# Four stacked graph layers on one core: another tile of each step goes to VectorE in layer 1, adjacency checks move from layer 1 to layer 3, constants are made one at a time, and layer 3's input relu goes to VectorE

## Chip, cores and metric

One core of one Trainium2 chip. The metric is device time in microseconds (us) of one launch; lower is better. Engines are named as the profile names them: PE is TensorE, with PEld for its weight loads; DVE is VectorE, ACT ScalarE, POOL GpSimd, SP SyncE, which here only issues DMAs.

## What is computed

The input is x (4096 rows of 64 features) and a dense float32 adjacency matrix adj (4096 x 4096, about one entry in a thousand is 1). Four layers, each `x = x + layer(relu(layernorm(x)), adj)`:

```
layer 0: h,q,k = lorentz linear maps;  att = adj * sigmoid((2 + 2 qm k^T)/scale + bias);  s = att h;  s / sqrt(|<s,s>|)
layer 1: w = mask * 0.5 ** (position counted from the row's last neighbour, the last 100 only);  w (h W) + bias
layer 2: 1 - 0.1 h - 0.01 * sum(h * (adj h))
layer 3: relu([h, (adj h) / max(deg, 1)] W^T)
```

## The kernel before

**Tiling.** Rows are in 32 tiles of 128; columns in 8 blocks of 512 (`NIB`), each with four row tiles (`CI`). The adjacency is loaded once as fp8 masks by POOL's DMA queue (`load_masks`, L186) and kept on chip for all layers. An fp8 mask is exact only if adj holds zeros and ones, so the kernel also reads adj again in float32 and checks it: `check` (L414) runs one VectorE instruction (L421) over a 128x1024 tile that SP's queue has fetched (L406; 512 KB, four buffers, so a tile is fetched once the check four before it is done). Layer 0 checks 60 tiles of half that size; 98 of full size remain for later. All must be done before `flagged` (L1237) sums the marks (`bad`, L1245), PE folds them over partitions (`pf`, L1249) and a flag decides whether a general version runs afterwards.

**Order.** The order of instructions on each engine is written out by hand. Epilogues of a block (`rows0`, `rows1`, `rows2`, `rows3`) are generators in a queue: `step` (L347) advances them piece by piece, and each engine runs what it is given strictly in that order. In layers 2 and 3, `beat` (L1499) runs after each four matmuls: a `step`, and a check if the list `often` says so for this beat.

**Layer 0** (0 to 297 us): scores on PE (L1015), sigmoids on ACT (L1028), masking on DVE (L1039), sums on PE (L1046). Early in it, `count_constants` (L896) makes the small matrices that layer 1 multiplies by (`after`, `beyond`, `pair`, `apart`, `later`, `lane`, `part`), mostly on POOL, in a burst of few pieces.

**Chunk counts** (297.9 to 314.7 us): `chunks_counted` (L1275) counts neighbours per block of rows on PE, for two halves of the columns. A dictionary says what is put in after which tile t: checks (`wide`), the three pieces of `weights_scaled` (L1292), and `all_taken`, which copies mask rows by SP's queue. `numbered` (L1346) then writes numbers into spare mask rows by DMA.

**Layer 1** (314.7 to 445.3 us): 264 units of one row tile and one column block, four to a step (k = 0 to 65), s = 0 to 3 in a step. For each step PE runs four `cnt` matmuls (L1391, in `counted`), then the four `acc` matmuls (L1423, in `products`) of the step before. Between them each `cnt` is rectified out of PSUM into int16, whose bits are the bf16 weights (`weights`, L1402): s = 1 by DVE (L1409; s = 3 too when k % 8 is 1), the others by ACT (L1411). The `cnt` tiles rotate through five PSUM banks, so unit n + 5 can only start once unit n is evacuated. After the products of a step comes a check if k is 4 or more and k % 5 is 0, 2 or 4, then a `step` for the epilogues.

**Layers 2 and 3** (445.3 to 511.7, then to the end): per layer 256 matmuls (L1509), each mask tile against features that are kept as a sum of two fp16 parts (`split`, L264). `rows2` (L1549) makes layer 3's input: it calls `norm` (L288) with `by_act`, where ACT takes the row sums (L296), the squares (L309) and the relu with its scale (L333, four instructions), before PE transposes (L1575). `rows3` (L1602) forms the output: ACT scales (L257), POOL adds twice (L261, L1617), DVE adds x (L1620), POOL issues the store (L1621).

The full-size checks by stage, counted from the code: 5 in the chunk counts, 38 in layer 1, 32 in layer 2, 23 in layer 3 (there one in three beats for the first 24 beats, then two in three).

Of the kernel before, what the change touches and what calls it, by code (L numbers as in the profile page):

```python
# [16 lines left out]
AF = mybir.ActivationFunctionType  # L17
# [9 lines left out]
P = 128  # L27
# [26 lines left out]
def kernel(  # L54
# [83 lines left out]
    def bc(col, r):  # L138

        return col.unsqueeze(2).to_broadcast([P, r, D])  # L140
# [4 lines left out]
    def model(general):  # L145
# [142 lines left out]
        def norm(rows, h, tag, table, up=UP, by_act=False):  # L288


            xr = x_sb[:, rows, :]
            st, va = small("st", tag), small("va", tag)
            sq = rows_tile("sq", tag)
            if by_act:
                for c in range(CI):
                    nc.scalar.activation(  # L296
                        sq[:, c, :], xr[:, c, :], AF.Copy, scale=-1.0 / D,
                        accum_out=st[:, c : c + 1],
                    )
            else:  # L300
                nc.vector.tensor_reduce(st, xr, AX.X, ALU.add)
                nc.vector.tensor_scalar(st, st, -1.0 / D, None, ALU.mult)  # L302
            yield
            xc = rows_tile("xc", tag)
            nc.gpsimd.tensor_tensor(xc, xr, bc(st, CI), ALU.add)  # L305
            yield
            if by_act:
                for c in range(CI):
                    nc.scalar.activation(  # L309
                        sq[:, c, :], xc[:, c, :], AF.Square, accum_out=va[:, c : c + 1]  # L310
                    )
            else:
                nc.scalar.activation(sq, xc, AF.Square)
                yield
                nc.vector.tensor_reduce(va, sq, AX.X, ALU.add)
            if table:
                yield
                rs = small("rs", tag)
                nc.scalar.activation(
                    rs, va, AF.Sqrt, bias=eps if up == 1.0 else eps_up, scale=1.0 / D / up / up  # L320
                )
                yield
                nc.vector.reciprocal(rs, rs)
            else:
                nc.vector.tensor_scalar(va, va, 1.0 / D / up / up, EPS / up / up, ALU.mult, ALU.add)
                rs = rsqrt(va, tag)
                yield
                yield
                yield
            h = xc if h is None else h  # L330
            if by_act:
                for c in range(CI):
                    nc.scalar.activation(  # L333
                        h[:, c, :], xc[:, c, :], AF.Relu, scale=rs[:, c : c + 1]
                    )
            else:
                nc.vector.scalar_tensor_tensor(h, xc, 0.0, bc(rs, CI), ALU.max, ALU.mult)
            yield
            return h

# [555 lines left out]
        def count_constants():  # L896
            tmp = epi.tile([P, 2, P], F32, tag="sup", name="tri")
            tri, diag = tmp[:, 0, :], tmp[:, 1, :]

            nc.gpsimd.memset(tri, 1.0)  # L900
            nc.gpsimd.affine_select(
                out=tri,
                in_=tri,
                compare_op=ALU.is_gt,
                fill=0.0,
                base=0,
                pattern=[[-1, P]],
                channel_multiplier=1,
            )
            nc.gpsimd.memset(part, 0.0)  # L910
            nc.gpsimd.memset(beyond, 0.0)
            nc.gpsimd.memset(pair, 0.0)
            nc.gpsimd.memset(apart, 0.0)
            nc.gpsimd.memset(later, 0.0)
            own = float(MAX_NEIGH * 128)
            for n in range(LANES):
                at = slice(n * NT, (n + 1) * NT)
                eye = ident[at, at]
                nc.gpsimd.tensor_scalar(pair[at, :], eye, 1.0, None, ALU.mult)
                nc.gpsimd.tensor_scalar(apart[at, at], eye, own, None, ALU.mult)  # L920
                if n > 0:
                    nc.gpsimd.tensor_scalar(apart[at, 0:NT], eye, -128.0, None, ALU.mult)
                yield
            yield
            yield
            nc.vector.tensor_scalar(diag, ident, float(MAX_NEIGH * 128), None, ALU.mult)
            nc.vector.scalar_tensor_tensor(after, tri, -128.0, diag, ALU.mult, ALU.add)
            nc.vector.memset(after[:, KEPT:P], 0.0)
            for q in range(QUAD):
                lanes = slice(q * NT, (q + 1) * NT)  # L930
                nc.gpsimd.tensor_scalar(beyond[lanes, lanes], tri[lanes, lanes], 1.0, None, ALU.mult)
                for n in range(LANES):
                    nc.gpsimd.tensor_scalar(
                        later[lanes, n * NT : (n + 1) * NT], tri[lanes, lanes], -128.0, None, ALU.mult
                    )
                nc.vector.memset(part[lanes, q : q + 1], 1.0)
            nc.vector.memset(lane, 0.0)
            nc.vector.memset(lane[:, NT - 1 : NT], 1.0)


        stream0 = pool("stream0", 1, l0) if general else None
# [460 lines left out]
        def weights(units, cnts, k):  # L1402


            ws = []
            for s, (cnt, (ib, t)) in enumerate(zip(cnts, units)):
                w = work1.tile([P, IB], I16, tag=f"w{s}", name=f"w_{ib}_{t}{sfx}", bufs=2)
                if s == 1 or (s == 3 and k % 8 == 1):
                    nc.vector.tensor_scalar(w, cnt, 0.0, None, ALU.max)  # L1409
                else:  # L1410
                    nc.scalar.activation(w, cnt, AF.Relu)  # L1411
                ws.append(w.bitcast(BF16))
            return ws

        with tc.manual_schedule():
# [34 lines left out]
            for _ in range(AHEAD):  # L1450
                fetch(2)
            chunks_counted(0, {
                0: wide, 2: scaled, 8: wide, 10: scaled,
                16: lambda: all_taken(range(QUAD, NIB)), 18: scaled, 22: wide,
            })
            chunks_counted(1, {4: lambda: numbered(0), 16: wide, 24: wide})
            if general:
# [6 lines left out]
            for blocks in GROUPS:  # L1464
                units = [(ib, t) for t in reversed(range(-1, NT)) for ib in blocks]
                for at in range(0, len(units), CI):
                    now = units[at : at + CI]
                    cnts = counted(now)
                    ws = weights(now, cnts, k)
                    if late is not None:  # L1470
                        products(*late)
                    late = now, ws
                    if k % 5 % 2 == 0 and k >= 4:
                        check(2)
                    k += 1
                    step()
                    if k == 4 and not general:
                        numbered(1)
                    if not moved and len(ready.get(1, ())) == NIB:
                        features_apart()  # L1480
                        moved = True
# [196 lines left out]
        with tc.manual_schedule():  # L1678
# [12 lines left out]
                for ib in range(NIB):  # L1691
                    degrees(ib)

            often[:] = [True, False, False]
            sums(3, s2a, v_sb3, done3, 4, 28)
            drain()
        l2.close()
# [55 lines left out]
```

## Time and profile before

| | us |
|---|---|
| median of 3 runs (585.33 to 585.69) | 585.34 |
| the profiled execution | 584.98 |
| its span | 583.2 |
| PE busy in the span | 558.3 (96%) |
| DVE / ACT / POOL busy | 461.7 / 364.6 / 256.7 |
| layer 1 (315 to 445): PE / DVE / ACT busy | 122.3 / 111.2 / 106.9 |

The span is the time from the first to the last instruction in the profile; 1.8 us lie around it. A group line names line, engine, operation, output and input, count, then busy time and mean ns, then the idle time of the engine just before, and what ended it. In a timeline, the first two numbers are start and busy time in us, and a bracket gives the idle time before it and its releaser. A matmul is shown as 0.38 us long, but back-to-back ones start 0.216 us apart: PE's idle in a bracket is 0.16 us less than what the wait costs.

### The profile page before, as it was taken

The numbers are of one execution on the slowest core, as the hardware profiler recorded it, in microseconds if no ns is written. First come the engines' busy times: TensorE is split into PE (matmuls) and PEld (weight loads), VectorE is DVE, ScalarE is ACT, GpSimd is POOL, SyncE is SP. The second block draws the span as 40 slices with busy tenths as digits, with TensorE's granted clock in tenths as the row PEclk, the third lists the DMA queues.
The fourth block names the chain that finished last, engine by engine and source line by source line (L and its number), as shares of the span: only waits on it lengthen the run. The fifth ranks groups of instructions, "written<-read, shape, count | busy, mean of one in ns | idle before, by whom it ended". The sixth has DMA issues, their size and how long they took to land.

```text
span 583.2 us, 8971 instructions
## 1 busy us (share of the span) xinstructions
PE 558.3 (96%) x2912; PEld 239.2 (41%) x2924; DVE 461.7 (79%) x867; ACT 364.6 (63%) x727; POOL 256.7 (44%) x483
## 2 busy tenths in 40 slices
PE   8999999999999999999989899999999999999995
PEld 3663333233333333333334345444444445444552
DVE  5779666788998999999965787979898888776742
ACT  3678667666776767667613788988784028863431
POOL 7625303976757575755346300201011336751360
PEclk9999999999999999999999999999999999999998
DMA  8995932699999999993243365545555797656921
GB/s 148 130 106 50 101 35 18 56 123 158 160 159 152 159 153 167 136 142 118 83 153 120 132 206 184 177 152 180 160 176 184 237 324 228 216 187 220 321 75 35
DMA packets 45417, 87.84 MB, mean 151 GB/s; under 512 B 6000, under 2 KB 24432, under 8 KB 45360
## 3 DMA queue, kind: packets, MB, share of 16 engines
q1 hardware_dynamic: 26112, 69.17, 36.2%
q0 software_dynamic: 18720, 17.57, 32.2%
q8 instruction: 25, 0.41, 0.3%
q10 hardware_dynamic: 528, 0.43, 0.3%
q14 instruction: 32, 0.26, 0.1%
HBM read 135.63 MB, written 1.05 MB: 234 GB/s over the span
## 4 chain that ended last, share of the span: by engine, by line
PE 57%; DVE 18%; POOL 9%; DMA 6%; ACT 5%; issue 4%; SPq 0%; ACTq 0%; DVEq 0%; POOLq 0%
PE acc L1046 14%; PE ps L1015 13%; PE acc L1509 9%; PE acc L1423 7%; PE cnt L1391 7%; DVE ckw L421 5%; DMA ckw<-adjt_dram 4%; DVE att L1039 3%; DVE w L1409 2%; POOL mask L186 1%; PE pt L247 1%; POOL s2a L267 1%; ACT ps L1028 1%; POOL xc L305 1%; DMA vec<-vecs_dram 1%
## 5 line engine op out<-in xcount | busy, mean ns | idle before, releaser
L421 DVE SCALAR_TENSOR_TENSOR ckw<-ckw 128x1024 f32<-128x1024 f32 x98 | 123.3, 1269 | 9.2 <-DMA ckw<-adjt_dram 5.4
L1015 PE MATMUL ps<-qt,kt 64*128 64x512 f32 x512 | 124.2, 611 | 4.1 <-DVE att L1039 3.1
L1046 PE MATMUL acc<-att,fb 128*64 128x512 f32 x512 | 117.8, 599 | 0.6 <-DVE att L1039 0.5
L1411 ACT ACTIVATE w<-cnt 128x512 int16<-128x512 f32 x184 | 97.1, 604 | 19.0 <-PE cnt L1391 18.1
L1039 DVE TENSOR_TENSOR att<-ps,mask 128x1024 f32<-128x1024 f32 x82 | 98.3, 1217 | 7.8 <-ACT ps L1028 7.8
L1028 ACT ACTIVATE ps<-ps,att_c,att_a 128x1024 f32<-128x1024 f32 x82 | 93.4, 1175 | 1.9 <-PE ps L1015 1.7
L1028 ACT ACTIVATE att<-ps,att_c,att_a 128x1024 f32<-128x1024 f32 x46 | 54.6, 1202 | 59.2 <-PE ps L1015 59.0
L186 POOL DMA_DIRECT2D mask<-adjt_dram x128 | 70.2, 560 | 19.5 <-DMA mask<-adjt_dram 17.6
L1015 PEld LDWEIGHTS ps<-qt,kt 64*128 64x128 f32 x512 | 44.8, 186 | 80.6 <-issue 33.5
L1391 PE MATMUL cnt<-mask,after 128*128 128x512 fp8e4 x256 | 67.1, 379 | 6.2 <-DVE w L1409 5.0
L1039 DVE TENSOR_TENSOR att<-att,mask 128x1024 f32<-128x1024 f32 x46 | 56.6, 1246 | 19.3 <-ACT att L1028 19.3
L1423 PE MATMUL acc<-w,s2a 128*128 128x512 bf16 x244 | 64.1, 379 | 1.5 <-ACT asb L231 0.8
L1046 PEld LDWEIGHTS acc<-att,fb 128*64 128x64 f32 x512 | 33.5, 136 | 73.0 <-issue 67.5
L305 POOL TENSOR_TENSOR xc<-x_sb,st 128x256 f32<-128x256 f32 x24 | 19.3, 802 | 95.8 <-DVE st L302 60.6
L1409 DVE TENSOR_SCALAR w<-cnt 128x512 int16<-128x512 f32 x72 | 48.5, 686 | 15.2 <-PE cnt L1391 14.9
L1509 PE MATMUL acc<-mask,s2a 128*128 128x512 fp8e4 x256 | 57.8, 379 | 0.0
L1509 PE MATMUL acc<-mask,s2b 128*128 128x512 fp8e4 x256 | 57.7, 379 | 0.0
L282 POOL TENSOR_TENSOR rs_a<-rs_y 128x4 f32<-128x4 f32 x48 | 19.1, 399 | 67.1 <-DVE rs_y L278 58.5
L421 DVE SCALAR_TENSOR_TENSOR ck<-ck 128x512 f32<-128x512 f32 x60 | 43.1, 719 | 0.0
L1391 PEld LDWEIGHTS <-after 128*128 128x128 bf16 x256 | 24.9, 99 | 36.6 <-issue 8.0
L1423 PEld LDWEIGHTS <-s2a 128*128 128x128 f16 x256 | 24.7, 98 | 31.5 <-issue 2.5
L1509 PEld LDWEIGHTS <-s2b 128*128 128x128 f16 x256 | 25.1, 98 | 27.1
(252 smaller groups left out, 633.3 us busy)
## 6 DMA issues: line engine op xcount, KB each, us to landing
ckw<-adjt_dram SPq DMA_DIRECT2D x98, 512.0 KB, 4.2
mask<-adjt_dram POOLq DMA_DIRECT2D x128, 128.0 KB, 8.5
ck<-adjt_dram SPq DMA_DIRECT2D x60, 256.0 KB, 5.6
x_sb<-x_dram SPq DMA_DIRECT2D x4, 256.0 KB, 7.6
out_dram<-y POOLq DMA_DIRECT2D x6, 128.0 KB, 2.4
apart_m<-mask SPq DMA_DIRECT2D x16, 16.0 KB, 3.9
mask<-apart_m SPq DMA_DIRECT2D x16, 16.0 KB, 4.8
out_dram<-y ACTq DMA_DIRECT2D x2, 128.0 KB, 2.1
```

The costliest lines, as they stand in the source:

```text
L186: nc.gpsimd.dma_start(out=masks[ib][:, g * CG : (g + 1) * CG, :], in_=adjt[ib, g])
L305: nc.gpsimd.tensor_tensor(xc, xr, bc(st, CI), ALU.add)
L421: nc.vector.scalar_tensor_tensor(at, at, 0.0, at, ALU.not_equal, ALU.not_equal, accum_out=odd[:, k : k + 1])
L1015: nc.tensor.matmul(ps[:, c, :], kt[half, g, :], qts[ib][half, :], start=True, stop=True)
L1028: nc.scalar.activation(to, ps, AF.Sigmoid, bias=att_c, scale=att_a)
L1039: nc.vector.tensor_tensor(att, frm, mask, ALU.mult)
L1046: nc.tensor.matmul(acc[c * D : (c + 1) * D, :], lhs[:, t, :], rhs[:, c, :], start=(at == 0), stop=(at == NG - 1), skip_group_check=True,)
L1391: nc.tensor.matmul(cnt, by, what, start=True, stop=True, skip_group_check=True)
L1409: nc.vector.tensor_scalar(w, cnt, 0.0, None, ALU.max)
L1411: nc.scalar.activation(w, cnt, AF.Relu)
L1423: nc.tensor.matmul(accs[ib], apart_s if t < 0 else both(s2a, t), w, start=(t == NT - 1), stop=False, skip_group_check=True,)
L1509: nc.tensor.matmul(acc, both(s2, t), masks[ib][:, t, :], start=(t == 0), stop=(t == NT - 1), skip_group_check=True,)
```

## The change

Six places. In layer 1, DVE takes s = 3 of each step and ACT the others (s = 1 goes to DVE too when k % 7 is 1). Layer 1 checks when k % 7 is 0, 2 or 4. In the chunk counts one check is left out, `all_taken` is put after tile 12 and the later two pieces of `weights_scaled` after tiles 20 and 28. Layer 3's first 24 beats check every second beat. `count_constants` yields after nearly every POOL instruction, takes `beyond` and `later` from `after`, and clears the last columns of `after` on POOL at its end. `norm` does the relu with its scale on DVE always (L337). Full-size checks by stage are then 4, 27, 32 and 35.

```diff
@@ norm
-            if by_act:
-                for c in range(CI):
-                    nc.scalar.activation(
-                        h[:, c, :], xc[:, c, :], AF.Relu, scale=rs[:, c : c + 1]
-                    )
-            else:
-                nc.vector.scalar_tensor_tensor(h, xc, 0.0, bc(rs, CI), ALU.max, ALU.mult)
+            nc.vector.scalar_tensor_tensor(h, xc, 0.0, bc(rs, CI), ALU.max, ALU.mult)
@@ count_constants
             nc.gpsimd.memset(part, 0.0)
-            nc.gpsimd.memset(beyond, 0.0)
-            nc.gpsimd.memset(pair, 0.0)
-            nc.gpsimd.memset(apart, 0.0)
-            nc.gpsimd.memset(later, 0.0)
+            yield
+            yield
+            yield
             own = float(MAX_NEIGH * 128)
+            nc.vector.tensor_scalar(diag, ident, own, None, ALU.mult)
+            nc.vector.scalar_tensor_tensor(after, tri, -128.0, diag, ALU.mult, ALU.add)
+            for q in range(QUAD):
+                lanes = slice(q * NT, (q + 1) * NT)
+                nc.vector.memset(part[lanes, q : q + 1], 1.0)
+            nc.vector.memset(lane, 0.0)
+            nc.vector.memset(lane[:, NT - 1 : NT], 1.0)
+            for to in (beyond, pair, apart, later):
+                yield
+                nc.gpsimd.memset(to, 0.0)
+            for q in range(QUAD):
+                at = slice(q * NT, (q + 1) * NT)
+                yield
+                nc.gpsimd.tensor_scalar(beyond[at, at], after[at, at], -128.0, None, ALU.is_equal)
+                for n in range(LANES):
+                    to = slice(n * NT, (n + 1) * NT)
+                    yield
+                    nc.gpsimd.tensor_scalar(later[at, to], after[at, at], 0.0, None, ALU.min)
             for n in range(LANES):
...
+                yield
                 nc.gpsimd.tensor_scalar(pair[at, :], eye, 1.0, None, ALU.mult)
+                yield
                 nc.gpsimd.tensor_scalar(apart[at, at], eye, own, None, ALU.mult)
                 if n > 0:
+                    yield
                     nc.gpsimd.tensor_scalar(apart[at, 0:NT], eye, -128.0, None, ALU.mult)
-                yield
-            yield
-            yield
...
+            yield
+            nc.gpsimd.memset(after[:, KEPT:P], 0.0)
@@ weights
-                if s == 1 or (s == 3 and k % 8 == 1):
+                if s == 3 or (s == 1 and k % 7 == 1):
                     nc.vector.tensor_scalar(w, cnt, 0.0, None, ALU.max)
@@ chunk counts
             chunks_counted(0, {
-                0: wide, 2: scaled, 8: wide, 10: scaled,
-                16: lambda: all_taken(range(QUAD, NIB)), 18: scaled, 22: wide,
+                0: wide, 2: scaled, 8: wide, 12: lambda: all_taken(range(QUAD, NIB)),
+                20: scaled, 28: scaled,
             })
@@ layer 1
-                    if k % 5 % 2 == 0 and k >= 4:
+                    if k % 7 in (0, 2, 4) and k >= 4:
                         check(2)
@@ before layer 3
-            often[:] = [True, False, False]
+            often[:] = [True, False]
             sums(3, s2a, v_sb3, done3, 4, 28)
```

## The prediction

> **What bounds the kernel now.** I read the busy shares first, then waits and timelines of the stretches that the change touches. PE is busy 96% and back to back from 60 us on but for short holes, so a microsecond counts where PE stands still, and nowhere else. The holes of layer 1, in the waits of 315 to 446 us:
>
> ```profile
> ACT w L1411 <- PE cnt L1391: 18.1, 44, 1.2
> DVE w L1409 <- PE cnt L1391: 14.9, 21, 2.5
> PE cnt L1391 <- DVE w L1409: 5.0, 7, 1.2
> ```
>
> Seven times PE waited for a tile that DVE evacuates, never for one of ACT's. With 0.16 us more each (pitch 0.216 against the 0.38 shown) that is 5.0 + 7 x 0.16 = 6.1 us. One of them in the timeline:
>
> ```profile
> 439.72 1.19 DVE L421 SCALAR_TENSOR_TENSOR ckw<-ckw 128x1024 f32<-128x1024 f32 x1
> ...
> 440.70 0.59 PE L1391 MATMUL cnt<-mask,after 128*128 128x512 fp8e4 x2
> 440.84 0.08 DVE L421 DVE_READ_ACCUMULATOR ckw<-ckw 128x1 f32 x1
> 440.84 0.42 DVE L337 SCALAR_TENSOR_TENSOR fa<-xc,rs 128x256 f32<-128x256 f32 x1
> 441.18 1.28 DVE L1409 TENSOR_SCALAR w<-cnt 128x512 int16<-128x512 f32 x2
> 441.18 0.60 ACT L1411 ACTIVATE w<-cnt 128x512 int16<-128x512 f32 x1 [0.64 <-PE cnt L1391]
> ...
> 441.91 0.59 PE L1391 MATMUL cnt<-mask,after 128*128 128x512 fp8e4 x2 [0.62 <-DVE w L1409]
> ```
>
> A check and an epilogue piece stand ahead of the evacuation on DVE; PE has two `cnt` and must wait for the bank of the third. The tail of the kernel, on DVE and PE:
>
> ```profile
> 556.82 0.43 DVE L1620 SCALAR_TENSOR_TENSOR y<-y,x_sb 128x256 f32<-128x256 f32 x1 [0.61 <-POOL y L1617]
> 557.17 1.22 DVE L421 SCALAR_TENSOR_TENSOR ckw<-ckw 128x1024 f32<-128x1024 f32 x1
> 558.31 0.08 DVE L421 DVE_READ_ACCUMULATOR ckw<-ckw 128x1 f32 x1
> 558.31 1.74 DVE L421 SCALAR_TENSOR_TENSOR ckw<-ckw 128x1024 f32<-128x1024 f32 x1
> 559.98 0.08 DVE L421 DVE_READ_ACCUMULATOR ckw<-ckw 128x1 f32 x1
> 560.66 0.43 DVE L1620 SCALAR_TENSOR_TENSOR y<-y,x_sb 128x256 f32<-128x256 f32 x1 [0.60 <-POOL y L1617]
> 563.53 0.42 DVE L1620 SCALAR_TENSOR_TENSOR y<-y,x_sb 128x256 f32<-128x256 f32 x1 [2.44 <-POOL y L1617]
> 563.88 0.41 DVE L1245 TENSOR_REDUCE bad<-odd 128x1 f32<-128x256 f32 x1
> ```
>
> And PE at the same time:
>
> ```profile
> 571.36 0.19 PE L1249 MATMUL pf<-one,bad 128*1 128x1 f32 x2
> 571.48 4.49 PE L1509 MATMUL acc<-mask,s2a 128*128 128x512 fp8e4 x20
> ```
>
> The last check ends at 560, `bad` at 564.3, and PE folds it at 571.36, with 20 matmuls behind it in its order. DVE is 7 us early.
>
> **Layer 1, the evacuations.** A `cnt` can be read about 0.47 us after its start (from 431.75 to ACT's start at 432.22, for one), DVE's evacuation takes 0.68, PE goes on 0.05 later: 1.20. Slot s = 1 gives its bank to the third `cnt` of the next step, nine matmuls on: 9 x 0.216 = 1.94, so DVE may be 0.74 late. Slot s = 3 is wanted first by its own product, twelve matmuls on: 2.59, so DVE may be 1.39 late. And of 38 checks (1.15 from start to start) 27 remain, no longer in consecutive steps: 12.7 us of DVE's 111 go. A step is 1.73 us; with one evacuation (0.60 from start to start), one check and a piece of 0.2 to 0.6 DVE is 0.2 to 0.6 late, inside 1.39. I let six of the seven waits go. At 414.9 ACT's evacuation of two finished sums (two of 0.70, to 415.4) is late next, and keeps 0.9 of that hole. Gain 6.1 - 0.9 = 5.2.
>
> The same move tightens ACT. Its three evacuations start 0.486 apart. Before it has slots 0, 2, 3; the tightest starts 0.06 late of an allowed 1.94 - 0.47 - 0.60 - 0.05 = 0.82. Now it has 0, 1, 2, and the third starts 2 x 0.486 - 2 x 0.216 = 0.54 late: 0.28 is left, and ACT regains 1.73 - 1.46 = 0.27 per step. What stands between its evacuations, in layer 1:
>
> ```profile
> L231 ACT ACTIVATE asb<-acc,level 128x512 f32<-128x512 f32 x8 | 5.1, 698 | 0.5 <-PE acc L1423 0.5
> L313 ACT ACTIVATE sq<-xc 128x256 f32<-128x256 f32 x7 | 3.0, 422 | 0.6 <-POOL xc L305 0.6
> L319 ACT ACTIVATE rs<-va,eps_up 128x4 f32<-128x4 f32 x6 | 1.9, 311 | 0.0
> L319 ACT ACT_TABLE_LOAD x1 | 1.3, 1283 | 0.0
> ```
>
> The table load with its root holds ACT from 365.26 to 366.76: evacuations 0.88 + 0.54 late of 0.82, a new hole of 0.6. Thirteen small pieces of 0.25 to 0.33 cost 0.05 each where alone, up to 0.3 where two meet or their input is late: 1.2 together. Three pairs of sums: 0.17 each, 0.5. So 2.3 comes back; bounds 0 (if DVE's better pace removes late inputs) and 4.7 (0.3 at each of twelve, 0.6, 0.5). Layer 1 by itself: 5.2 - 2.3 = **2.9 gained**, bounds 5.2 and 0.5.
>
> The row of the table load bears on a page: the Trainium skill, "ScalarE: Activation LUTs", section "What ACT_TABLE_LOAD costs", gives 1283 ns for the load and some 1380 ns of drain. Here the root starts 0.02 us after the load's end, so no drain shows; with one the new hole would be 2.0 and the layer's gain 1.5, and I go by the row.
>
> **Chunk counts.** PE stood still 0.97 us before `pw` (L1299) at 302.13, because DVE made `wn_size` only after a check that waited for its tile (to 301.86). With `pw` after tile 20, forty matmuls of 0.054 = 2.2 us later, its input is there. The chain behind it (counts, numbers, mask DMA to 316.3) moves along: SP's queue, free from 306.8, waits for DVE's numbers at 309.8, and `all_taken` leaves it earlier, not later. The left-out check ended at 306.1, before DVE was wanted. **1.0 gained**, bounds 1.3 and 0.2 (if the DMAs land no earlier).
>
> **Constants.** In layer 0 the burst sits on POOL from 104.7 to 108.5 and 110.9 to 116.2. ACT waited 2.97 us for `xc` (L305) behind its first part, and PE stood 0.73 + 0.16 before the scores at 111.95; DVE waited 2.04 for POOL's root behind the second, and PE lost 1.19 + 0.16 at 127.58 and some 0.6 in between. Singly, each piece (0.28, some 0.85) stands ahead of one mask DMA (0.56); masks are loaded some 20 tiles ahead, so that costs nothing unless a root is delayed, which could open one of the 0.8 us holes that later blocks show (180.97, 211.91, 242.86). **1.6 gained**, bounds 2.6 and -0.5.
>
> **The relu.** ACT's four take 1.07 (514.69 to 515.76), after a hop from DVE's reciprocal; on DVE, right behind it, one of 0.42 (the row of L337). Eight of them on DVE, 3 us, fit: DVE is busy 52 of 66 us in layer 2. On PE's path are only the transposes at 502.6 (0.47) and 515.3 (0.83 + 0.16, 0.15, and 0.25 for ACT's `asb` behind the relus). **1.0 gained**, bounds 1.5 and -0.6 (half a check ahead of it).
>
> **The moved checks.** Layer 3 has 35 instead of 23. Four more in its first 24 beats fit into DVE's idle time (3.6 us before 534.6, 1.4 before the first `y` at 549.1). The `y` of L1620 come 3.84 us apart while two checks stand between them (552.98, 556.82, 560.66), because POOL's add takes 1.59 beside a check and 0.72 alone. The changed order has two more after the `y` of 560.66, so the next is at 564.5; then seven in a row; then a `y`, and only then `bad`. From 564.85: 7 x 1.15 + 0.52 (one is stretched to 1.74 beside POOL) = 573.4; `y` 0.35, `bad` 0.41, hop 0.1: PE folds at 574.3 instead of 571.36, 2.9 late, and 20 matmuls wait. The tiles' DMAs can add: a load starts when the check four before has ended and lands 4.7 us later (median of 536 to 560; least 3.2), so the last check starts not before 568.8 + 4.7 = 573.5, and the hole is 4.2. I take **3.4 lost**, bounds 2.5 and 4.3.
>
> A page bears on the stretched rows too: "SBUF — State Buffer", section "Who interferes with whom", says that a DVE instruction with two SBUF inputs and a GpSimd one that reads SBUF exclude each other, and the later one is blocked outright. Here both lengthen (1.22 to 1.74 and 0.72 to 1.59). If only POOL paid, the hole would be 0.5 smaller.
>
> **Sum.** -2.9 - 1.0 - 1.6 - 1.0 + 3.4 = -3.1: 584.98 becomes 581.9 for an execution like the profiled one. The median lies 0.36 above it: **582.2**.
>
> **Rivals.**
> 1. The flag is not late (0.12): DVE's idle time in layer 3 before `bad` (3.8 before 534.6, 1.4, three of 0.6, 2.4: 9.4 us) takes nearly all twelve. For: 12 x 1.15 = 13.8 is only half again that. Against: most of the idle time lies before the order lets the last seven begin. 582.2 - 3.4 = 578.8.
> 2. ScalarE becomes layer 1's bound (0.17): its holes take what DVE's gave. For: 0.28 us of room. Against: no PE wait for ACT's `cnt` before. 582.2 + 2.9 = 585.1.
> 3. Slower (0.16): the late flag takes more than all gains. The place is `pf`; the price is 1.15 us for each check still open behind the `y` at 564.5. If the four extra checks of the first 24 beats are not absorbed, eleven are open, and the hole is 3.4 + 4 x 1.15 = 8.0: 582.2 + 4.6 = 586.8. It decides from a hole of 6.5, the sum of the gains. Against: 5 us of idle time in that stretch.
>
> **Numbers.** Forecast 0.55, rivals 0.12, 0.17, 0.16. Faster by over 0.2% (below 584.2; about what a measurement of this kernel can tell from no change): 0.55 + 0.12 = 0.67; within it 0.17; slower 0.16. All bounds at their best give 582.2 - 5.0 = 577.2, at their worst 590; leaving a tenth out on each side I say 578.5 to 586.8.
>
> **What would show it.** Right: PE's waits for DVE's `w` fall from 5.0 us to under 1, waits for ACT's `w` appear, one beside the table load; no hole at `pw`; ACT's `xc` wait near 110 gone; a hole of 2.5 to 4.3 before `pf`, and seven checks in a row ahead of `bad`. Wrong: no hole before `pf`, or PE waiting for ACT in most steps of layer 1.

## The result and the profile after

The changed kernel takes 589.67 us (median of 4 runs, 589.33 to 592.34), the kernel before 585.52 beside it: ratio 1.0080, 95% interval 1.0065 to 1.0094. The forecast was 582.2, with a range up to 586.8. The profiled execution took 589.73, its span 588.0, 4.8 longer than before. Stage times, here and below, are those of the one profiled execution of a kernel; where it lies far from the kernel's median, that is said. By stage, from the first matmul of each on PE (us):

| | before | after | difference | predicted |
|---|---|---|---|---|
| layer 0 ends at | 297.90 | 300.17 | +2.3 | -1.6 (constants) |
| chunk counts | 16.80 | 15.76 | -1.0 | -1.0 |
| layer 1 | 130.66 | 129.39 | -1.3 | -2.9 |
| layer 2 | 66.38 | 65.30 | -1.1 | -1.0 (relu, with the next row) |
| layer 3 until PE reaches `pf` | 59.53 | 58.47 | -1.1 | |
| PE idle ahead of `pf` | 0.09 | 5.60 | +5.5 | +3.4 |
| `pf` to the start of the last matmul | 4.23 | 5.72 | +1.5 | 0 |
| from there to the end of the span | 7.65 | 7.58 | -0.1 | 0 |

In what follows checks stand at L415 of the changed kernel, the rest of layer 1 where it stood. First layer 1, in the waits of 315 to 446 us:

```profile
DVE w L1409 <- PE cnt L1391: 28.9, 31, 2.9
ACT w L1411 <- PE cnt L1391: 16.6, 41, 1.5
...
PE acc L1423 <- ACT asb L231: 1.2, 6, 0.2
PE cnt L1391 <- ACT w L1411: 0.4, 1, 0.4
PE acc L1423 <- DVE w L1409: 0.2, 1, 0.2
PE cnt L1391 <- DVE w L1409: 0.2, 1, 0.2
```

DVE now waits for PE twice as long as before, and PE's waits for DVE's `cnt` fell from 5.0 to 0.2 us. Six waits for ACT's sums and one for ACT's `w` stand in their place; that one is beside the table load, where the prediction put it, and 0.36 long as shown (0.53 from start to start, with two of 0.27 behind it, where one of 0.6 was foretold). The timeline:

```profile
365.81 1.28 ACT L319 ACT_TABLE_LOAD   x1
...
367.11 0.30 ACT L319 ACTIVATE rs<-va,eps_up 128x4 f32<-128x4 f32 x1
...
367.31 3.02 ACT L1411 ACTIVATE w<-cnt 128x512 int16<-128x512 f32 x6
...
367.94 1.35 PE L1391 MATMUL cnt<-mask,after 128*128 128x512 fp8e4 x3 [0.36 <-ACT w L1411]
```

The tail, on DVE:

```profile
563.17 0.42 DVE L1620 SCALAR_TENSOR_TENSOR y<-y,x_sb 128x256 f32<-128x256 f32 x1 [0.61 <-POOL y L1617]
...
566.33 1.73 DVE L415 SCALAR_TENSOR_TENSOR ckw<-ckw 128x1024 f32<-128x1024 f32 x1
...
569.60 1.23 DVE L415 SCALAR_TENSOR_TENSOR ckw<-ckw 128x1024 f32<-128x1024 f32 x1 [0.39 <-DMA ckw<-adjt_dram]
...
571.52 1.22 DVE L415 SCALAR_TENSOR_TENSOR ckw<-ckw 128x1024 f32<-128x1024 f32 x1 [0.69 <-DMA ckw<-adjt_dram]
...
574.23 0.41 DVE L1245 TENSOR_REDUCE bad<-odd 128x1 f32<-128x256 f32 x1
```

And on PE:

```profile
574.69 0.19 PE L1249 MATMUL pf<-one,bad 128*1 128x1 f32 x2 [5.43 <-DVE bad L1245]
574.81 5.98 PE L1509 MATMUL acc<-mask,s2a 128*128 128x512 fp8e4 x20
```

Seven checks stand between the `y` and `bad`, as foretold, but they take longer, and the 20 matmuls behind `pf`, which took 4.49 before, take 5.98. The windows show the second (PE busy first; the granted clock is the third number from the end):

```profile
150.00:152.50 2.50, 1.87 (x6) 0.95 (x8) 2.50 (x5) 1.47 (x3) 2.08 (x6) 0.74 1.12 106
152.50:155.00 2.50, 2.50 (x10) 0.91 (x8) 1.99 (x4) 1.91 (x2) 2.07 (x7) 0.58 0.71 219
...
575.00:577.50 2.50, 2.50 (x7) 0.91 (x6) 0.91 (x3) 0.00 (x0) 0.90 (x2) 0.50 0.17 59
```

PE is busy all through 575 to 577.5, with 7 matmuls instead of 13: it runs at half its clock. In the kernel before the clock is 1.00 in every stretch of 2.5 us between 60 and 570 us. The other low stretch, near 150 us, lies behind the loss of layer 0:

```profile
140.06 0.69 POOL L922 TENSOR_SCALAR beyond<-after 32x32 bf16<-32x32 bf16 x1
...
140.81 0.60 POOL L186 DMA_DIRECT2D mask<-adjt_dram  x1
141.49 0.93 POOL L926 TENSOR_SCALAR later<-after 32x32 bf16<-32x32 bf16 x1
...
145.02 0.32 POOL L933 TENSOR_SCALAR apart<-ident 32x32 bf16<-32x32 f32 x1
145.27 0.64 POOL L305 TENSOR_TENSOR xc<-x_sb,st 128x256 f32<-128x256 f32 x1
...
145.94 0.42 ACT L313 ACTIVATE sq<-xc 128x256 f32<-128x256 f32 x1 [4.47 <-POOL xc L305]
...
148.73 1.13 PE L1015 MATMUL ps<-qt,kt 64*128 64x512 f32 x4 [2.06 <-DVE att L1039]
```

Five constant pieces, a mask DMA issue ahead of each, are queued on POOL in front of the centred rows `xc`: 5.9 us from the first issue at 139.37 to `xc`. In the kernel before five mask issues stand there alone, 2.7 us, and `xc` starts 0.64 earlier (144.63) although PE ran 2.7 us behind:

```profile
141.93 2.72 POOL L186 DMA_DIRECT2D mask<-adjt_dram  x5
...
145.33 0.42 ACT L313 ACTIVATE sq<-xc 128x256 f32<-128x256 f32 x1 [1.19 <-POOL xc L305]
```

In the changed kernel ACT's square waits for `xc`, the next sigmoids wait behind the square in ACT's order, DVE's masking waits for them, and PE stands still. Up to 138 us PE was those 2.7 us ahead of the kernel before; here it loses them and more: the hole and a second of 0.77 at 150.6 cost 3.2 us (with 0.16 more each), and the low clock behind them some 1.7 (2.5 us at 0.74 and 2.5 at 0.58).

**Theory** after these traces: constants made singly delay `xc` in a block of layer 0; seven checks behind the fifth `y` delay the flag; and a PE that stood idle is given half the clock for some microseconds afterwards, so a long hole costs more than itself. In layer 1 the thinner checks gain, and the move of the slot costs. **Rivals:** the holes of layer 0 come from the mask issues and not from the constants; the slot's move is free, or is itself the gain; the clock falls by its place in the program; the loss in the tail is one of DMA bandwidth, whatever the order.

### The profile page after: what moved, and what is told of

Its sections match the earlier page's. It is cut to its first block, busy times and chain, and to the rows that moved or that the text cites. A ratio compares the mean times of both kernels' runs of the same rounds, so it can differ in the third digit from the quotient of the medians.

```text
span 588.0 us, 8935 instructions
## 1 busy us (share of the span) xinstructions
PE 562.1 (96%) x2924; PEld 240.0 (41%) x2924; DVE 467.9 (80%) x872; ACT 357.8 (61%) x697; POOL 259.3 (44%) x484
## 3 DMA queue, kind: packets, MB, share of 16 engines
HBM read 135.63 MB, written 1.05 MB: 232 GB/s over the span
## 4 chain that ended last, share of the span: by engine, by line
PE 54%; DVE 16%; POOL 11%; DMA 8%; ACT 5%; issue 5%; SPq 0%; POOLq 0%; ACTq 0%; DVEq 0%
PE acc L1046 13%; PE ps L1015 12%; PE acc L1423 8%; PE cnt L1391 8%; PE acc L1509 6%; DVE att L1039 4%; DVE ckw L415 3%; DMA ckw<-adjt_dram 3%; POOL mask L186 2%; POOL x_sb L1566 2%; PE many L1280 1%; POOL prod L261 1%; POOL xc L305 1%; DMA ck<-adjt_dram 1%; DMA vec<-vecs_dram 1%
## 5 line engine op out<-in xcount | busy, mean ns | idle before, releaser
L415 DVE SCALAR_TENSOR_TENSOR ckw<-ckw 128x1024 f32<-128x1024 f32 x98 | 124.2, 1278 | 9.5 <-DMA ckw<-adjt_dram 5.8
L1411 ACT ACTIVATE w<-cnt 128x512 int16<-128x512 f32 x183 | 95.8, 604 | 17.2 <-PE cnt L1391 16.6
L1391 PE MATMUL cnt<-mask,after 128*128 128x512 fp8e4 x256 | 68.4, 379 | 2.3 <-DMA mask<-two 1.2
L1423 PE MATMUL acc<-w,s2a 128*128 128x512 bf16 x256 | 66.4, 379 | 1.4 <-ACT asb L231 1.2
L1509 PE MATMUL acc<-mask,s2a 128*128 128x512 fp8e4 x256 | 59.2, 386 | 0.0
L282 POOL TENSOR_TENSOR rs_a<-rs_y 128x4 f32<-128x4 f32 x48 | 17.7, 369 | 66.4 <-DVE rs_y L278 58.3
L415 DVE SCALAR_TENSOR_TENSOR ck<-ck 128x512 f32<-128x512 f32 x60 | 42.7, 712 | 0.0
L1423 PEld LDWEIGHTS <-s2a 128*128 128x128 f16 x256 | 24.6, 97 | 34.3 <-issue 6.9
L1509 PEld LDWEIGHTS <-s2a 128*128 128x128 f16 x256 | 25.0, 99 | 28.4 <-issue 1.9
```

The lines of the kernel that those rows point to most:

```text
L415: nc.vector.scalar_tensor_tensor(at, at, 0.0, at, ALU.not_equal, ALU.not_equal, accum_out=odd[:, k : k + 1])
L1391: nc.tensor.matmul(cnt, by, what, start=True, stop=True, skip_group_check=True)
L1423: nc.tensor.matmul(accs[ib], apart_s if t < 0 else both(s2a, t), w, start=(t == NT - 1), stop=False, skip_group_check=True,)
L1509: nc.tensor.matmul(acc, both(s2, t), masks[ib][:, t, :], start=(t == 0), stop=(t == NT - 1), skip_group_check=True,)
```

## Experiments

### Parts taken out of the change

**Constants in a burst, as before**, all else changed.

```diff
-(count_constants of the change)
+(count_constants of before)
```

> The changed kernel with the constants made in a burst again, as before the change. Theory A (in layer 0 the single constant pieces stand on POOL ahead of a block's xc, ACT waits 4.5 us for it, PE loses 4.9 us with the slower clock after it): the hole near 148 us goes, the two smaller ones near 112 and 127 come back (2.7 us), layer 0 ends at 297.9 instead of 300.2, and the time is about 587.4. Rival (the hole comes from the clock dip at 150 us, or from PE running 2.7 us ahead, whatever POOL does): a hole of 3 us or more stays near 150 us and the time is 589 or more.

Measured: 589.22 (588.99 to 590.38), ratio 1.0077 (1.0060 to 1.0094). ACT's wait of 4.47 and the hole near 148 are gone and the clock stays at 1.00 there; layer 0 ends at 298.77, 1.4 earlier. But PE then comes to `pf` earlier, the hole there is 6.55 instead of 5.60, and the medians differ by only 0.45, which the intervals don't tell from nothing. While the flag is late, the cure of layer 0 hardly shows.

**Checks as before**, all else changed.

```diff
-                    if k % 7 in (0, 2, 4) and k >= 4:
+                    if k % 5 % 2 == 0 and k >= 4:
-            often[:] = [True, False]
+            often[:] = [True, False, False]
```

> The changed kernel with layer 1's and layer 3's checks as before the change (38 and 24). Theory B (the twelve moved checks make the fold pf late by 5.6 us, and PE then runs its last 20 matmuls at half clock for another 1.4): the hole before pf is under 1 us and layer 3 is 6 to 7 us shorter; layer 1 gets some DVE waits back, 1 to 3 us; the time is 584 to 586. Rival (the moved checks cost nothing by themselves, layer 3 is longer because the relu now stands on DVE): the hole stays, about 589.

Measured: 588.15 (583.42 to 589.44, 10 runs), ratio 1.0024 (1.0001 to 1.0047). The hole ahead of `pf` is 0.09 and the matmuls behind it take 4.24: both losses of the tail go with the checks. But layer 1 takes 134.01, 4.6 more than in the change: one wait for DVE of 2.08 at 338.95, and behind it a low clock that costs 1.7. The profiled execution took 589.44, 1.3 above the median, and the ten lie far apart, so how often the wait comes is open; 584 to 586 was expected.

**The fold behind the last matmul** (PE issues `pf` five steps later).

```diff
-            for _ in range(steps):
+            for _ in range(steps + 5):
                 yield
             pf = pm.tile(...)
```

> The changed kernel, but PE folds the marks (pf) after its last matmul of layer 3 instead of 20 matmuls before; all checks stay where the change put them. Theory B (the cost is PE standing at pf): the matmuls of layer 3 end 6.5 to 7 us earlier, the time is 583 to 584. Rival (the checks' loads or DVE's lateness set the end themselves): the tail waits for DVE instead and the time is 587 or more.

Measured: 586.43 (584.98 to 589.59), ratio 1.0027 (1.0009 to 1.0045). The last matmul starts 8.8 us earlier, 1.75 of it from layer 0, but the rest from there takes 12.87 instead of 7.58: the last evacuations on ACT and DVE stand behind the flag in their order. From the start of layer 3 to the end the change takes 5.9 us more than the kernel before, and this one 3.9 more: a third of the loss was PE standing ahead of work that it could do, the rest is the flag itself. The time is short of the 583 to 584 foretold.

**More of the moved checks early in layer 3**: two beats in three from its start.

```diff
-            often[:] = [True, False]
+            often[:] = [True, True, False]
```

> The changed kernel with two checks in three beats from the start of layer 3 on (16 instead of 12 in the first 24 beats), so that about three instead of seven stand ahead of bad after the y of block 4. Theory B: each of the four costs 1.2 to 1.5 us at the end, so the hole before pf shrinks from 5.6 to about 0.5 us, the clock stays up, and the time is 583 to 585, if the first 24 beats have room on DVE. Rival (no room there: DVE or the loads are full, the lateness is only passed on): the hole stays over 3 us, 587 to 590.

Measured: 588.05 (586.64 to 589.16), ratio 1.0057 (1.0040 to 1.0073). The hole falls only to 3.47: between 529 and 556 DVE waits ten times for a tile, 5.2 us in all. Two of them, on DVE:

```profile
543.95 1.29 DVE L415 SCALAR_TENSOR_TENSOR ckw<-ckw 128x1024 f32<-128x1024 f32 x1 [1.05 <-DMA ckw<-adjt_dram]
...
556.15 1.48 DVE L415 SCALAR_TENSOR_TENSOR ckw<-ckw 128x1024 f32<-128x1024 f32 x1 [1.08 <-DMA ckw<-adjt_dram]
```

So the rival holds for a part: with two checks in three beats the tiles are late. Whether that is the DMA's bandwidth or the wait for a free one of the four buffers was not told apart; the DMA share from 529 to 556 is 0.91 here and in the change, 0.81 before.

### Parts put into the kernel before

**Constants alone.**

```diff
-(count_constants of before)
+(count_constants of the change)
```

> The kernel before with the constants made one at a time, and nothing else. Theory A: layer 0 loses the two holes near 112 and 127 us (2.7) and gets one near 148 (4.9 with the slow clock): about +2.2, 587.6. Rival (the hole needs other parts of the change): -2 to 0, 583 to 585.5.

Measured: 586.52 (585.31 to 589.18), ratio 1.0028 (1.0012 to 1.0044). The profiled execution has the wait of 4.45 at the square, the hole of 2.06 on PE and a clock of 0.68, 0.50 and 0.50 from 150 to 157.5; layer 0 ends at 302.62. That execution took 589.18, 2.7 above the median. The step that was to gain 1.6 loses 1.6 by itself, going by the ratio. How much depends on the clock: the six profiles with these constants end layer 0 at 298.42 and 298.59 where the clock stays up behind the holes, and at 299.64 to 302.80 where it falls, against 297.85 to 298.96 in the nine with the burst.

**The relu alone.**

```diff
-            if by_act: (four nc.scalar.activation)
-            else: nc.vector.scalar_tensor_tensor(h, xc, 0.0, bc(rs, CI), ALU.max, ALU.mult)
+            nc.vector.scalar_tensor_tensor(h, xc, 0.0, bc(rs, CI), ALU.max, ALU.mult)
```

> The kernel before with layer 3's input relu on DVE, and nothing else. If the relu is what made layers 2 and 3 up to pf 2.2 us shorter in the changed kernel: 583.3. If it was the thinner DVE queue at the end of layer 1: 585.0 to 585.5.

Measured: 582.54 (582.32 to 583.95), ratio 0.9959 (0.9946 to 0.9972). Layer 2 is 1.23 shorter, layer 3 1.05. In the timeline of the kernel before, on ACT and PE:

```profile
501.95 1.06 ACT L333 ACTIVATE sup<-xc,rs 128x64 f32<-128x64 f32 x4 [1.16 <-DVE rs L323]
502.59 0.81 PE L1575 MATMUL ph<-ident,sup 128*128 128x128 f32 x2 [0.31 <-ACT sup L333]
```

And with the relu on DVE:

```profile
500.95 0.52 DVE L331 SCALAR_TENSOR_TENSOR sup<-xc,rs 128x256 f32<-128x256 f32 x1
...
501.62 0.41 PE L1569 MATMUL ph<-ident,sup 128*128 128x128 f32 x2
```

The transposes find their input and PE doesn't wait. Layer 1, where no instruction differs, is 0.66 shorter here, 0.57 of it in the wait for the spare mask rows' DMA, and 0.07 shorter in another kernel with this edit: so much one profile differs from another.

**The slot alone.**

```diff
-                if s == 1 or (s == 3 and k % 8 == 1):
+                if s == 3 or (s == 1 and k % 7 == 1):
```

> The kernel before with DVE on the fourth tile of a step (and the second when k % 7 is 1), checks as before. If the later slot is what ended DVE's waits in layer 1: PE's waits for DVE's w fall below 2 us, ACT's tighter turn gives about 4 back, 584 to 585. If it was the eleven checks taken out of layer 1: DVE's waits stay, ACT's come on top, 587 or more.

Measured: 587.87 (586.92 to 589.70), ratio 1.0044 (1.0027 to 1.0061). In the profiled execution (589.70, 1.8 above the median) layer 1 takes 134.39, 3.7 more. PE's waits for DVE's `cnt` fall from 5.0 to 2.1, but that is one wait:

```profile
333.40 1.23 DVE L421 SCALAR_TENSOR_TENSOR ckw<-ckw 128x1024 f32<-128x1024 f32 x1 [1.87 <-DMA ckw<-adjt_dram]
...
334.89 1.28 DVE L1409 TENSOR_SCALAR w<-cnt 128x512 int16<-128x512 f32 x2
...
335.63 0.92 PE L1391 MATMUL cnt<-mask,after 128*128 128x512 fp8e4 x2 [2.10 <-DVE w L1409]
```

A check whose tile is late holds up DVE, with two evacuations behind it; and behind PE's wait the clock is 0.65 and 0.67 from 335 to 340, which costs another 1.7. The kernel with the checks of before and all else changed has the same wait at 338.95 and the same fall of the clock.

**The checks alone.**

```diff
-                    if k % 5 % 2 == 0 and k >= 4:
+                    if k % 7 in (0, 2, 4) and k >= 4:
-            often[:] = [True, False, False]
+            often[:] = [True, False]
```

> The kernel before with layer 1's checks thinned (k % 7) and layer 3's taken every second beat at first, as in the change, and nothing else; with the one check that the change leaves out of the chunk counts still there, 34 fall to layer 3. Layer 1 gains 2 to 4 us from a freer DVE. Theory B: the fold is late by 3 to 5 us and the slow clock costs 1.4 more: 586 to 589. Rival (the late fold needs the relu on DVE as well): 582 to 584.

Measured: 588.04 (586.75 to 589.25), ratio 1.0056 (1.0034 to 1.0078). Layer 1 takes 127.23, 3.4 less, with DVE still on its old slot; PE's waits for DVE's `cnt` are 1.5 instead of 5.0. The gain of layer 1 is that of the checks. The tail takes it back: a hole of 3.15 ahead of `pf`, and 5.92 instead of 4.23 behind it.

### Which version, and the clock by itself

**Relu and chunk counts in the kernel before.**

> The kernel before with two parts of the change: the relu of layer 3 on VectorE, and the new table of duties in the chunk counts (one check fewer there). Constants, layer 1 and its checks as before. Theory (the parts add up): the relu alone measured 0.9959 of before (2.4 to 2.9 us), the chunk counts took 15.76 instead of 16.80 us in every kernel that has the new table; the check that leaves them sits at the end, where the last check of before ended some 5 us ahead of the flag's multiply. So 2.5 + 1.0: 581.9 us if before is 585.4, no hole at the flag's multiply. Rival (the chunk's gain is taken back by the longer row of checks): 582.9, the same as the relu alone, with a hole ahead of the flag's multiply.

Measured: 582.04 (581.49 to 583.35), ratio 0.9946 (0.9932 to 0.9959). The chunk counts take 15.76, 1.0 less; by the ratios the pair gains 0.8 us on the relu alone, and 581.9 was expected. Within that the parts add up.

**With them, layer 1's checks thinned as in the change and put into layer 2.**

```diff
-        made, beats, often = [0], [0], [True, False]
+        made, beats, often = [0], [0], [True, True, False]
-                    if k % 5 % 2 == 0 and k >= 4:
+                    if k % 7 in (0, 2, 4) and k >= 4:
```

> The kernel before with the relu on VectorE, the new table in the chunk counts, and the thinner checks in layer 1 (three beats in seven), the displaced ones put into layer 2 at two beats in three instead of one in two; layer 3's checks as before, so none is issued behind the fifth y. The tile that VectorE evacuates in layer 1 stays the second; constants as before. Theory (the thin checks are the gain in layer 1, and the flag is late only because the displaced checks stand in layer 3): layer 1 takes about 127 us (130.0 in the relu kernel, 127.2 with thin checks alone), no hole ahead of the flag's multiply, the last 20 matmuls in about 4.2; layer 2 pays 0 to 1.5 us. Time 578.5 to 581 us. Rival (VectorE is the bound of layer 2 too, 24.5 of 30 us busy there): layer 2 pays what layer 1 gains, 3 us, and the time stays at 581.5 to 582.5.

Measured: 592.48 (591.10 to 593.22), ratio 1.0126 (1.0111 to 1.0140). Layer 1 takes 128.06, of which 0.86 are four matmuls of layer 2 that the profile shows ahead of its last product: 127.2, 3.4 less than without the move. No hole stands ahead of `pf`; but layer 2 takes 75.11 instead of 65.29. The theory left this out, and the rival was far too mild. Where it is lost first:

```profile
478.35 0.17 DVE L1558 TENSOR_SCALAR inn<-inn 128x4 f32<-128x4 f32 x1
...
480.15 0.26 ACT L296 ACTIVATE sq<-x_sb 128x64 f32<-128x64 f32 x1 [6.12 <-POOL x_sb L1560]
...
481.12 0.67 ACT L231 ACTIVATE asb<-acc,level 128x512 f32<-128x512 f32 x1
...
481.84 1.11 PE L247 MATMUL pt<-ident,asb 128*128 128x128 f32 x4 [4.18 <-ACT asb L231]
```

Five checks in a row (469.81 to 477.5, one of them with a tile 1.01 late) stand ahead of `inn`; POOL's new x waits for `inn`, ACT idles 6.12 before its row sums, and the evacuation PE waits for stands behind these in ACT's order. From 480 to 487.5 the clock is 0.57, 0.50 and 0.57. Layer 2 has no room for so many checks. Later holes of this kernel, of 1.99 at 501.4 and 2.48 at 522.5, are followed by the full clock.

**Matmuls that fill the wait ahead of `pf`.** The changed kernel with 24 more matmuls, whose result nothing reads:

```diff
+            fill = pm.tile([P, IB], F32, tag="pr", name="fill")
+            for _ in range(24):
+                nc.tensor.matmul(fill, both(s2a, 0), masks[0][:, 0, :], start=True, stop=True, skip_group_check=True)
             pf = pm.tile(...)
```

> The changed kernel with 24 matmuls of 128x512 more, whose result nothing reads, issued just ahead of the flag's multiply (about 5.2 us of TensorE work at the full clock); all else is as in the change. The flag stays as late as it is, but TensorE doesn't stand idle while it waits. Theory (idle time ahead of the flag lowers the granted clock, and so costs more than itself): the hole of 5.6 us is filled for the most part, the 20 matmuls behind the flag's multiply take 4.2 to 4.6 us instead of 5.98, no clock of 0.50 is seen there, and the time is 1.0 to 1.6 us below the changed kernel's. Rival (the clock falls by something else than the idle time, such as the place in the program): the 20 matmuls take 5.9 again, and the time is that of the changed kernel or higher by what the fillers overhang.

Measured: 588.90 (588.70 to 591.19), ratio 1.0067 (1.0052 to 1.0083). The profile of PE, and below it that of the windows:

```profile
568.62 5.34 PE L1250 MATMUL fill<-mask,s2a 128*128 128x512 fp8e4 x24
575.50 0.19 PE L1255 MATMUL pf<-one,bad 128*1 128x1 f32 x2 [1.54 <-DVE bad L1245]
575.62 4.49 PE L1515 MATMUL acc<-mask,s2a 128*128 128x512 fp8e4 x20
```

```profile
575.00:577.50 2.50, 2.00 (x11) 1.01 (x12) 1.30 (x5) 0.00 (x0) 1.29 (x2) 1.00 0.16 56
577.50:580.00 2.50, 2.50 (x13) 0.98 (x10) 0.04 (x1) 0.00 (x0) 0.00 (x0) 1.00 0.19 62
```

The program differs only in that PE is busy, and stands idle 1.54 instead of 5.43 as shown; the 20 matmuls take 4.49 at the full clock: it is the idle time that lowers it, not the place in the program. A check's tile came 1.71 late in this profile, and the flag with it (65.36 us from the start of layer 3 to `pf` instead of 64.07), so that of the 1.5 us saved behind `pf` 0.2 is left; another 0.5 by which the profile is shorter lies in layer 0. The medians differ by 0.8, where 1.0 to 1.6 was foretold.

**Single constants at half the pace**, in the kernel before: each `yield` of the new `count_constants` stands twice.

> The kernel before with the constants made singly as in the change, but one in every second step instead of in each, so that about half as many pieces and mask issues stand on GpSimd ahead of a block's centred rows; all else as before. Theory (the pieces and the mask issues between them hold up the centred rows, and so ScalarE and TensorE): of the wait of 4.5 us that ScalarE had at the square near 145 us at least 1.5 us goes, the hole on TensorE there falls from 2.7 to below 1.5 us, the granted clock stays at full speed behind it, and layer 0 ends at 295.5 to 297.5 us (297.9 before, 302.6 with a piece in every step): time 583.0 to 585.0. Rival (another cause than the pieces, for instance the mask issues alone): hole and end of layer 0 stay as with a piece in every step, 298.5 or later.

Measured: 586.72 (586.06 to 590.28), ratio 1.0027 (1.0015 to 1.0039); in the profiled execution (590.28, 3.6 above the median) layer 0 ends at 303.47. The theory's times were wrong, its mechanism not: ACT's wait near 145 falls from 4.45 to 2.15 and PE's hole there to 0.77, but pieces are now left for the next block:

```profile
177.74 0.60 POOL L186 DMA_DIRECT2D mask<-adjt_dram  x1
...
178.41 0.60 POOL L305 TENSOR_TENSOR xc<-x_sb,st 128x256 f32<-128x256 f32 x1
...
179.05 0.42 ACT L313 ACTIVATE sq<-xc 128x256 f32<-128x256 f32 x1 [5.04 <-POOL xc L305]
...
181.84 1.24 PE L1031 MATMUL ps<-qt,kt 64*128 64x512 f32 x4 [2.69 <-DVE att L1055]
```

The hole moved from 149 to 181 us with the pieces; the clock behind it is 0.55, 0.50 and 0.59 from 182.5 to 190. In the kernel before no piece is left by then, and that block's hole is 0.62. Five mask issues stand ahead of `xc` with and without the pieces, and the hole comes with the pieces: so the pieces make it. What the issues add to it was not tried apart.

**Half of the checks moved**: relu, chunk counts, and a check at every second step of layer 1 (31 instead of 38), the rest in layer 3.

```diff
-                    if k % 5 % 2 == 0 and k >= 4:
+                    if k % 2 == 0 and k >= 4:
-            often[:] = [True, False, False]
+            often[:] = [True, False]
```

> The kernel before with the relu on VectorE and the new table in the chunk counts (the pair that measured 0.9946), and layer 1's checks at every second step from the fourth on (31 instead of 38), no two in consecutive steps; layer 3's first 24 beats check every second beat, as in the change. Slots and constants as before. Three checks are then left behind the fifth y and the sixth y no longer stands ahead of the marks' sum, against seven and a y in the change. Theory (VectorE's waits in layer 1 go with the checks, and each check behind the fifth y costs TensorE 1.15 us once the slack of the flag is used up): layer 1 about 128.5, the hole ahead of the flag's multiply 5.6 - 4 x 1.15 - 0.35 = 0.6, no low clock behind it; against the pair's 582.04, 2.0 less in layer 1 and 0.5 more at the flag: 580.5. Rival (the moved checks load the DMA queues too, and the last tiles land late whatever their number): the hole is 2 to 3 us, the clock falls behind it, and the time is 583 to 584.

Measured: **579.60** (578.90 to 580.21), ratio 0.9892 (0.9874 to 0.9910): 1.1% faster than before. Layer 1 takes 127.93. On DVE and PE:

```profile
563.18 1.74 DVE L415 SCALAR_TENSOR_TENSOR ckw<-ckw 128x1024 f32<-128x1024 f32 x1
...
564.96 0.42 DVE L1239 TENSOR_REDUCE bad<-odd 128x1 f32<-128x256 f32 x1
```

```profile
566.09 0.19 PE L1243 MATMUL pf<-one,bad 128*1 128x1 f32 x2
566.21 4.49 PE L1503 MATMUL acc<-mask,s2a 128*128 128x512 fp8e4 x20
```

Three checks behind the fifth `y`, none of them waiting for its tile; `bad` is ready 0.7 us before PE comes to `pf`.

**The change without the slot and the constants.**

> The change without its two parts that are held to have lost: VectorE keeps the second tile of a step in layer 1, and the constants stay in their burst. It has the thin checks in layer 1, the denser ones in layer 3, the table of the chunk counts and the relu on VectorE. Beside the kernel that has the change but for the constants it tells the move of the slot by itself. Theory (the slot's move costs in layer 1 because ScalarE's three consecutive tiles leave it no room): layer 1 takes 127.0 to 128.1 instead of 129.3, the hole ahead of the flag's multiply stays at 5 to 6.5 us with a low clock behind it, and the time is 585.5 to 588. Rival (the slot's move is free, the loss lies in the late flag and the clock alone): layer 1 takes 129 to 130.

Measured: 586.79 (585.16 to 588.71), ratio 1.0019 (1.0005 to 1.0032). Layer 1 takes 126.52, against 129.30 in the kernel that differs by the slot alone (the first experiment): a difference of 2.8. Of that 0.7 is PE's wait for the spare mask rows' DMA (0.45 here, 1.15 there), so the move costs 2.1; the other kernels with thin checks and the old slot, where that wait is 1.16 and 1.12, took 127.2 both, 2.1 less than 129.30. The hole ahead of `pf` is 6.45 and the clock 0.50 behind it:

```profile
570.37 0.19 PE L1243 MATMUL pf<-one,bad 128*1 128x1 f32 x2 [6.29 <-DVE bad L1239]
570.49 6.95 PE L1503 MATMUL acc<-mask,s2a 128*128 128x512 fp8e4 x20
```

## Why the prediction was wrong

The predicted sum was -3.1, the profile has +4.8. The 7.9 between them, from the table of stages:

1. **"Singly, each piece ... stands ahead of one mask DMA ...; ... so that costs nothing unless a root is delayed"** failed: 3.9 of the 7.9 (+2.3 for -1.6). The gains came (2.7 us by 138), but the new holes cost 3.2 and the clock behind them some 1.7, and what was delayed is no root. It is `xc`, for which ACT had waited 2.97 in the very row that the prediction read. The pieces meet the next `xc` instead, with a mask issue between each two, and hold it for 4.47. The bound of 0.5 for a loss was taken from existing holes of 0.8 and not from the length of the queue.
2. **The moved checks: mechanism right, size wrong**: 2.1 (5.5 for 3.4). The `y`s came 3.84 apart and seven checks stood in a row, as foretold. But PE came 0.9 nearer, since the relu shortens PE's part of layer 3 and not the chain of the `y`s; and the checks took 10.4 us from the last `y` instead of 8.6, two stretched beside POOL for one, and two late tiles (0.39 and 0.69). The late tile was in the prediction's bound of 4.3, PE's approach was not. The prediction took its rows of a check and POOL's add for "both lengthen", as if against the rule that the later one is blocked; in order of time these rows fit that rule. POOL's add at 564.48 runs to 565.32, the check of 564.66 ends at 566.40, the next add (565.39) at 566.98 and the next check (566.33) at 568.06, each some 0.6 (add) or 1.1 (check) behind the end of the one before: so a check pays for each add begun before it, and two adds stretched two checks. The third rival ended on the right side by luck: its four extra checks were absorbed (seven in the row, not eleven), and it kept the other steps' gains.
3. **The clock behind the hole was left out**: 1.5 here, beside the 1.7 in point 1. "20 matmuls wait" was priced as if they ran at 0.216 us each afterwards. The filling shows that the price is the idle time's. The kernel before has no hole on PE of over 1.22 us from 60 us to the flag, and no low clock there, so its profile gave no warning.
4. **Layer 1**: 1.6 (-1.3 for -2.9). The waits went as foretold: from start to start, less 0.216, PE's holes at `cnt` behind a DVE evacuation fell by 5.1 us, and 5.2 was said. What was mis-sized is "So 2.3 comes back": 3.7 came back, 2.6 of it at `cnt` behind ACT (ten holes of 0.15 or more end right behind an ACT evacuation, 2.3 us; none in the kernel without the slot's move), the rest at the products. And the gain belongs elsewhere: "Slot s = 3 ... may be 1.39 late" was to end six waits together with the thinner checks, but the thin checks alone bring 5.0 down to 1.5. The move of the slot costs 2.1 more than it takes from the rest. With the checks of before it costs more in the one profile (+3.7), by one late tile and the clock behind it.
5. **The relu** was better than said: 2.1 for 1.0 (layers 2 and 3 in the change), 2.3 alone. Set side by side matmul by matmul, the profile with the relu alone gains 1.5 at the two places that the prediction read (502.6, and 515.3, where a wait of 0.94 stays), 0.3 at the transposes of 522.3, and 0.45 at two waits for ACT's `ht` (492.6 and 505.3) that it had not counted.
6. **The chunk counts** were right: 1.0, in every kernel with the new table.

Points 1 to 5 together: 3.9 + 2.1 + 1.5 + 1.6 - 1.1 = 8.0.

The page "TensorE: Matmul & The Clock Gate" of the Trainium skill, section "Why this matters for your kernels", advises against idle gaps of over some 3 us between bursts of matmuls. The flag's hole of 5.6 agrees (clock 0.50 behind it); below that the traces show both outcomes, as the last section tells.

## What to carry to other kernels

An engine's small work that is spread out doesn't become free: look what is queued behind each new place, and follow it to PE, before it is costed at nothing. A part of a change that gains can be paid for by another (checks out of layer 1, checks into the tail), so price the two ends apart and move only as much as the far end's slack takes: here moving 7 checks of 38 made 582.04 into 579.60, moving 11 made it 586.79. And add to a hole on PE the half clock that can follow it, here for 3.4 or 6.8 us, so 1.7 or 3.4 us of loss: it followed every hole of 3.15 us or more, some of 2.0 to 2.7, and no shorter one before PE's last matmuls.

## What was not expected of the hardware

A hole on PE was followed by a granted clock of 0.50, at times at less than 3 us of idle time: in every profile with 3.15 us or more (3.15 to 6.55 ahead of `pf`, 4.3 in layer 2), in both with 2.1 shown at 335 and 339 us, after the 2.69 at 181.84, and in four of six with the one of 2.06 and 0.77 near 150; in the other two (298.42 and 298.59 at the end of layer 0) no stretch there fell below 0.93, nor did one behind the 1.99 and 2.48 in the kernel with more checks in layer 2. So between 2.0 and 2.7 us the length of the hole does not settle it.

The traces show what does. Within a profile the clock changes only at times that lie whole multiples of 3.41 us apart (in the changed kernel at 151.19, 154.61, 574.45, 577.86 and 584.69), and it stays at 0.50 for one or two such stretches. Over the 16 profiles, from 60 us on, it fell behind every stretch of this grid at the full clock in which PE was shown idle for 2.0 us or more, behind none with less than 1.5, and between 1.5 and 1.8 it went either way. The holes of 2.06 and 0.77 show it. With the constants alone the first lies within one stretch (busy 1.33 of 3.42 us), and the clock falls at its end; with more checks early in layer 3 the border runs through it (two stretches, idle 1.73 and 1.10), and the clock stays up:

```profile
147.46:150.88 3.42, 1.33 (x6) 0.30 (x4) 2.37 (x5) 3.42 (x4) 1.40 (x5) 1.00 1.10 157
```

```profile
145.04:148.46 3.42, 1.69 (x8) 0.30 (x4) 0.95 (x1) 2.46 (x3) 2.57 (x7) 1.00 1.10 112
148.46:151.87 3.41, 2.31 (x10) 0.99 (x12) 3.34 (x8) 2.81 (x5) 1.85 (x6) 1.00 1.12 145
```

The hole of 2.48 is likewise split, into stretches with 1.28 and 1.20 of idle time. This was read from the traces alone; no run moved a hole against the grid on purpose.
